# First attention of a Flamingo block: the later queries as seven half-size products instead of eight, with streamed weight sums

## Chip, cores and metric

The kernel runs on one core of one Trainium2 chip. TensorE multiplies matrices into PSUM; VectorE, ScalarE and GpSimd do the elementwise work; SP issues most DMAs. The metric is the device time of one execution in microseconds, as the median of several.

## What is computed

The reference is a two-layer gated block on x, 16 batches of 128 tokens by 512 features, all fp32. Only its first attention matters here:

```python
x = x + jnp.tanh(g_xattn[0]) * _L0_xattn_ref(_layernorm(x), ctx_512, ...)
...
q_hk = (hidden_q @ Wq.T).reshape(b, s, H, K)           # H = 16 heads
q_big = jnp.einsum('bshk,hkq->bshq', q_hk, w_kc_q)
kv_rope = kv_c * cos[None] + _rotate_half(kv_c) * sin[None]
q_r = jnp.einsum('bshq,hqr->bhsr', q_big, W_qr)        # R = 64
k_r = jnp.einsum('bld,hdr->bhlr', kv_rope, W_kr)
scores = jnp.einsum('bhsr,bhlr->bhsl', q_r, k_r)
```

Then come a softmax, the weighted sum of kv_rope, the projection back to x, a mixture-of-experts feed-forward layer, a causal attention and a second feed-forward layer.

## The kernel before

**Folding.** Up to 73 us the three query weights are multiplied into one matrix `fq` in SBUF: 4 blocks of 128 input features by 1024 columns, one column for each head and rank. The 1024 columns are 8 pairs of heads of 128 columns; `fq[:, c, ts(p, P)]` is the block of feature chunk c and head pair p. In the same way the outward weights are folded later (`fold_next`, 78 to 97 us) into `fo_raw` and `fo_sums`.

**Pairs of batches.** The 16 batches are taken as 8 pairs v = 0 to 7. The queries of pairs 0 and 1 are made during the folding with 512 tokens at a time. Those of pairs 2 to 7 come from `keys_and_queries(v)` with 256 tokens, the two batches of the pair side by side: for each of four j, two head pairs of queries (`query`, 4 matmuls of 256 columns each), the copy out of PSUM, two head pairs of keys (`key`), and their copy. `normalise` makes the normalised x, `turn` transposes it by TensorE into `turned[g]`, which two pairs share.

**Order.** Pair 2 is made in the prelude, in pieces between softmax steps. Then the loop over units u = 1 to 8 does for pair v = u-1: `gather` (weighted sums), `project` (seven products, already in the seven-product form with its sums `pair_sums`, `fo_sums`), and for pair u: `score`, `soften` (exponentials on ScalarE, scaling on GpSimd at L703), `block` (VectorE's block transposes) and `carry` (16 DMAs on SP that finish the transposition). In units 2 to 6 `keys_and_queries(u + 1)` comes last, and the next unit's `gather` and `score` follow it on TensorE. `combine_next` prepares feed-forward weights in every unit: loads and stores on SP, four sums on GpSimd (L826).

**What sets the order.** From `ordered[0] = pinned[0] = True` on, every matmul, every `send` and every VectorE instruction inside `pin` stays in program order on its engine. ScalarE's, GpSimd's and unpinned instructions, and DMAs that those engines issue, are placed by the compiler's scheduler. Each engine runs its own queue in order, so an instruction that waits holds up those behind it.

**Memory.** PSUM tiles have 512 fp32 columns; `mm_tile` has 4 buffers, `tr_tile` 2, `acc_tile` 2. Before, queries use `tr_tile`, keys `acc_tile`, scores `mm_tile`. `evacuate` alternates between VectorE (L85) and ScalarE (L87).

Of the kernel before, what the change touches and what calls it, by code (L numbers as in the profile page):

```python
# [9 lines left out]
F32 = mybir.dt.float32  # L10
AF = mybir.ActivationFunctionType
ALU = mybir.AluOpType
# [3 lines left out]
P = 128  # L16
NB = 16
D = 512
ND = D // P
GB = 4  # L20
NG = NB // GB
GT = GB * P
H = 16
NPAIR = H // 2
R = 64
# [17 lines left out]
def kernel(  # L43
# [9 lines left out]
    nc = tc.nc  # L53
# [4 lines left out]
    lnp = ctx.enter_context(tc.tile_pool(name="lnp", bufs=2))  # L58
# [16 lines left out]
    def pin(ins):  # L75
        if pinned[0]:
            tc.keep_in_program_order(ins)
# [3 lines left out]
    def evacuate(dst, src):  # L81

        flip[0] ^= 1
        if flip[0]:
            pin(nc.vector.tensor_copy(dst, src))  # L85
        else:
            nc.scalar.copy(dst, src)  # L87
# [40 lines left out]
    fq = wp.tile([P, ND, H * R], F32, tag="w16", name="fq")  # L128
# [39 lines left out]
    def matmul(*args, **kw):  # L168
        ins = nc.tensor.matmul(*args, **kw)  # L169
        if ordered[0]:  # L170
            tc.keep_in_program_order(ins)

    def transpose(*args):
        ins = nc.tensor.transpose(*args)
        if ordered[0]:
            tc.keep_in_program_order(ins)
# [29 lines left out]
    half = GT // 2  # L206
    lo, hi = slice(0, half), slice(half, GT)
    bp = ctx.enter_context(tc.tile_pool(name="f0b", bufs=1))
    wd = ctx.enter_context(tc.tile_pool(name="wd", bufs=1, space=bass.MemoryType.DRAM))
# [168 lines left out]
    with tc.tile_pool(name="a0", bufs=2) as ap, tc.tile_pool(name="a0s", bufs=3) as sp:  # L378
# [31 lines left out]
        def key(dst, p, kvT):  # L410
            matmul(dst, wkr_sb[:, ts(p, P)], kvT, start=True, stop=True)

        def query(dst, p, xnT):
            for c in range(ND):
                matmul(
                    dst, fq[:, c, ts(p, P)], xnT[:, c, :],
                    start=(c == 0), stop=(c == ND - 1),
                )

        def homes(what, v):  # L420
            twos = [
                ap.tile([P, 2, 2 * P], F32, tag=f"{what}{j}", name=f"{what}_{v}_{j}", bufs=1)
                for j in range(NPAIR // 2)
            ]
            return [t[:, i, :] for t in twos for i in range(2)], twos

        normal, xns, turned = {}, {}, {}
# [21 lines left out]
                xns[v].append(xn)  # L449

        def turn(v, which=(0, 1)):
            g, h = divmod(v, 2)
            if h == 0 and which[0] == 0:
                turned[g] = lnp.tile([P, ND, GT], F32, tag="xnT", name=f"xnT_a0_{g}", bufs=1)
            for i in which:
                xn = xns[v][i]
                tr = (acc_tile if v == 2 else tr_tile)(f"xtr_a0_{v}_{i}")
                for c in range(ND):
                    transpose(tr[:, ts(c, P)], xn[:, ts(c, P)], ident)
                dst = turned[g][:, :, ts(2 * h + i, P)]  # L460
                if v == 2:
                    pin(nc.vector.tensor_copy(dst, tr.rearrange("p (c t) -> p c t", t=P)))
                else:
                    evacuate(dst, tr.rearrange("p (c t) -> p c t", t=P))

        kvr_0 = kvT_0 = xnT_0 = None
        k_r, q_r = {0: homes("k", 0)[0]}, {0: homes("q", 0)[0]}
        for kept, tag in ((k_r, "ca"), (q_r, "cb")):  # L470
            t = ap.tile([P, NPAIR, 2 * P], F32, tag=tag, name=f"{tag}_kq", bufs=1)
# [3 lines left out]
        with tc.tile_pool(name="fold", bufs=3, side="right") as fp:  # L475
# [85 lines left out]
            for p in range(NPAIR):  # L561
# [27 lines left out]
                q_ps = tr_tile(f"q_ps0_{p}")  # L589
# [19 lines left out]
        rp = right_pools.enter_context(tc.tile_pool(name="a0r", bufs=2, side="right"))  # L609
# [57 lines left out]
        def score(b):  # L667


            v, i = divmod(b, 2)  # L670
            tiles = [mm_tile(f"s_ps{b}_{t}") for t in range(4)]
            for p in range(NPAIR):
                for j in range(2):
                    rows = slice(j * R, (j + 1) * R)
                    matmul(
                        tiles[p // 4 * 2 + j][:, ts(p % 4, P)],
                        q_r[v][p][rows, ts(i, P)], k_r[v][p][rows, ts(i, P)],
                        start=True, stop=True,
                    )
            ebs[b] = rp.tile([P, NK, H, BK], F32, tag="eb", name=f"eb_{b}")  # L680
            eTs[b] = rp.tile([P, NK, H, BK], F32, tag="eT", name=f"eT_{b}")
            soft[b] = []
            for t in range(4):
                nmx = sp.tile([P, 4], F32, tag="nmx", name=f"nmx_a0_{b}_{t}", bufs=4)
                pin(nc.vector.tensor_reduce(  # L685
                    nmx, tiles[t].rearrange("p (i l) -> p i l", l=P), AX.X, ALU.max,
                    negate=True,
                ))
                soft[b].append((tiles[t], nmx))

        def soften(b, t):
# [14 lines left out]
            soft[b][t] = e3  # L706

        def block(b, t):
            pin(nc.vector.transpose(
                ebs[b][:, :, 4 * t : 4 * t + 4, :].rearrange("p k n i -> p n k i"),  # L710
                soft[b][t].rearrange("p n (k i) -> p n k i", k=NK),
            ))
# [43 lines left out]
        def project(v, n):  # L756
# [17 lines left out]
            for i, cols in targets:  # L774
# [2 lines left out]
                    dst, y_ps, gate_x[0], dst, ALU.mult, ALU.add  # L777
                ))

        def keys_and_queries(v):  # L780
            g, h = divmod(v, 2)
            half = slice(2 * h * P, (2 * h + 2) * P)
            (k_r[v], k_two), (q_r[v], q_two) = homes("k", v), homes("q", v)
            for j in range(NPAIR // 2):
                q_ps = tr_tile(f"q_ps{v}_{j}")
                for i in range(2):
                    query(q_ps[:, ts(i, 2 * P)], 2 * j + i, turned[g][:, :, half])
                evacuate(q_two[j], q_ps.rearrange("p (i t) -> p i t", i=2))
                k_ps = acc_tile(f"k_ps{v}_{j}")
                for i in range(2):  # L790
                    key(k_ps[:, ts(i, 2 * P)], 2 * j + i, roped[g][1][:, half])
                evacuate(k_two[j], k_ps.rearrange("p (i t) -> p i t", i=2))
                yield j


# [61 lines left out]
        ups = {}  # L857

        xk = [wd.tile([P, D], F32, name=f"xk_{n}") for n in range(KEPT)]
        ordered[0] = pinned[0] = True  # L860


        def fold_next(p):
            fold_outward(p, outward[p])
            if p + 5 < NPAIR:
                outward.append(load_outward(p + 5))

        score(0)
        for p in range(7):
            fold_next(p)  # L870

            if p in (3, 5):
                turn(2, (p // 2 - 1,))
            if p % 2 == 0:
                soften(0, p // 2)
                if p:
                    block(0, p // 2 - 1)
        score(1)
        fold_next(7)
        block(0, 3)  # L880
# [3 lines left out]
        soften(1, 1)  # L884
        block(1, 0)
        pairs_2 = keys_and_queries(2)
        for t in (2, 3):
            next(pairs_2)
# [18 lines left out]
        for u in range(1, last + 1):  # L907
# [3 lines left out]
            v = u - 1  # L911
# [16 lines left out]
            if u == 1:  # L928
                now = odd
            else:  # L930
                gather(2 * v)
                if u < last:
                    score(even)
                if u + 1 < last:
                    if u % 2:
                        latents((u + 1) // 2)
                    turn(u + 1)
                if u < last - 1:
                    combine_next()
                elif u == last - 1:  # L940
                    turn_blocks(first)
# [609 lines left out]
    q = first  # L1551
    for g in range(NG):
# [40 lines left out]
        q = nxt  # L1593
# [34 lines left out]
    ap = ctx.enter_context(tc.tile_pool(name="l1", bufs=2))  # L1628
# [6 lines left out]
    for s in range(AHEAD, NB + AHEAD):  # L1635
# [38 lines left out]
        if s in (3, 5, 7):  # L1674
            n = s // 2 - 1
# [6 lines left out]
    g = NG - 1  # L1682
# [87 lines left out]
```

## Time and profile before

| what | us |
|---|---|
| median of 3 runs | 1499.63 (1497.9 to 1499.63) |
| the profiled execution | 1500.14 |
| its span, first to last instruction | 1498.3 |
| TensorE busy (granted clock 0.998) | 1477.4 |
| q_ps matmuls of 256 columns, 384 instructions, mean 379 ns, busy time | 86.9 |
| k_ps matmuls of 256 columns, 96 instructions, busy time | 24.6 |
| TensorE idle between 90 and 130 | 0.89 |
| TensorE idle between 230 and 260 | 0.00 |
| moved by DMA: SP's queue 157.13 MB, ScalarE's 0.99 MB, GpSimd's 4.13 MB | |

PE is TensorE's matmuls, PEld its weight loads, DVE VectorE, ACT ScalarE, POOL GpSimd, SPq SP's issues. L169 is the helper through which nearly all matmuls go, so groups are told apart by their tiles: `q_ps<-xnT_a,fq` are the queries. Matmul durations overlap; the time that one costs is the distance between starts. An idle time and what ended it stand in brackets. In a row of the DMA list the last number is the time from issue to landing.

### The profile page before, as it was taken

The page shows a single profiled execution, that of the slowest core. Times are in us where ns is not written, and L with a number is a line of the kernel's source. Part 1 is how long each engine was busy: PE and PEld are TensorE (multiplying, and loading weights), DVE is VectorE, ACT ScalarE, POOL GpSimd, SP SyncE. Part 2 cuts the span into 40 slices and gives each one's busy share as a digit, 9 for nine tenths or more (in the row PEclk, how much of TensorE's full clock was granted, in tenths as well). Part 3 has the DMA queues.
Part 4 walks back from the last instruction along what each step waited for, and adds up shares of the span by engine and source line. Part 5 has one row for each costly group of instructions (what it writes and reads, how often), then busy time and mean ns, then how long its engine had stood idle before and what let it go on. Part 6 is the DMA issues. An engine that isn't in the chain of part 4 may idle for free. (4 is left out here: it accounts for less than half of the span.)

```text
span 1498.3 us, 19508 instructions
## 1 busy us (share of the span) xinstructions
PE 1477.4 (99%) x6752; PEld 997.9 (67%) x6752; DVE 832.9 (56%) x1722; ACT 436.9 (29%) x1432; POOL 466.5 (31%) x500
## 2 busy tenths in 40 slices
PE   7999999999999999999999999999999999999999
PEld 5567778778877666876678666876668444444444
DVE  2274644654656555655564656455556776757422
ACT  1262432432441122012210321022203565545310
POOL 1153533623422233204320442124414333324200
PEclk9999999999999999999999999999999999999999
DMA  7533645344244822452246222721242342323212
GB/s 265 144 94 94 188 140 153 111 119 125 64 81 139 249 74 74 122 151 74 74 113 159 74 74 72 197 90 63 80 136 71 76 127 71 84 61 90 64 29 99
DMA packets 142274, 163.50 MB, mean 109 GB/s; under 512 B 54096, under 2 KB 102224, under 8 KB 140000
## 3 DMA queue, kind: packets, MB, share of 16 engines
q1 hardware_dynamic: 139024, 157.13, 36.5%
q0 software_dynamic: 2016, 4.13, 1.1%
q8 instruction: 54, 0.88, 0.3%
q10 hardware_dynamic: 1136, 0.99, 0.2%
q14 instruction: 44, 0.36, 0.1%
HBM read 106.35 MB, written 18.09 MB: 83 GB/s over the span
## 5 line engine op out<-in xcount | busy, mean ns | idle before, releaser
L1130 POOL TENSOR_TENSOR near<-base,a 128x512 f32<-128x512 f32 x32 | 42.6, 1332 | 345.0 <-ACT base L1127 233.5
L201 POOL TENSOR_TENSOR e<-e,rden_a 128x512 f32<-128x512 f32 x64 | 66.6, 1040 | 164.5 <-DVE rden_a L199 141.8
L169 PE MATMUL q_ps<-xnT_a,fq 128*128 128x256 f32 (+1 forms) x448 | 115.8, 410 | 0.0
L1127 ACT ACTIVATE a<-a 128x512 f32<-128x512 f32 x64 | 40.3, 630 | 256.8 <-DVE a L1126 256.8
L169 PE MATMUL l_ps<-t,b_sb 128*128 128x512 f32 x256 | 115.1, 592 | 0.0
L696 ACT ACTIVATE e<-s_ps,nmx_a 128x128 f32<-128x128 f32 x256 | 90.2, 386 | 78.0 <-DVE nmx_a L685 40.4
L194 ACT ACTIVATE e<-e,nmx_a 128x128 f32<-128x128 f32 x256 | 98.8, 387 | 34.7 <-DVE nmx_a L189 34.7
L1126 DVE TENSOR_TENSOR a<-l_ps,base 128x512 f32<-128x512 f32 x64 | 44.0, 688 | 108.0 <-PE l_ps L169 107.9
L169 PEld LDWEIGHTS q_ps<-xnT_a,fq 128*128 128x128 f32 x448 | 84.8, 190 | 24.5 <-issue 12.5
L703 POOL TENSOR_TENSOR e<-e,rden_a 128x512 f32<-128x512 f32 x64 | 66.0, 1039 | 100.7 <-DVE rden_a L701 100.7
L169 PEld LDWEIGHTS l_ps<-t,b_sb 128*128 128x128 f32 x256 | 48.6, 190 | 59.5 <-issue 57.6
L169 PE MATMUL fy_ps<-ring,far 128*128 128x256 f32 x384 | 87.2, 380 | 0.0
L169 PE MATMUL y_ps<-fo_raw,c 128*128 128x256 f32 x384 | 85.8, 380 | 0.9 <-DVE c L85 0.9
L776 DVE SCALAR_TENSOR_TENSOR x<-y_ps,gates,x 128x256 f32<-128x256 f32 x112 | 48.7, 477 | 67.0 <-PE y_ps L169 66.9
L1192 DVE SCALAR_TENSOR_TENSOR x<-fy_ps,gw,x 128x256 f32<-128x256 f32 x112 | 46.5, 475 | 69.3 <-PE fy_ps L169 69.3
L169 PEld LDWEIGHTS fy_ps<-ring,far 128*128 128x128 f32 x384 | 72.6, 190 | 13.6 <-issue 4.0
L169 PEld LDWEIGHTS y_ps<-fo_raw,c 128*128 128x128 f32 x384 | 72.3, 190 | 10.7 <-ACT c L87 1.0
L1344 DVE STREAM_TRANSPOSE eb<-e 128x512 f32<-128x512 f32 x64 | 45.5, 712 | 42.0 <-POOL e L201 37.4
L169 PE MATMUL ht_ps<-T,ring 128*128 128x256 f32 x256 | 65.7, 379 | 0.0
L169 PE MATMUL t_ps<-a,a_sb 128*128 128x512 f32 x128 | 65.4, 592 | 0.0
L169 PE MATMUL t_ps<-base,a_sb 128*128 128x512 f32 x128 | 65.4, 592 | 0.0
L169 PE MATMUL y_ps<-fo_sums,c 128*128 128x256 f32 x256 | 60.4, 385 | 2.1 <-ACT c L87 0.8
(257 smaller groups left out, 2956.3 us busy)
## 6 DMA issues: line engine op xcount, KB each, us to landing
ring<-w SPq DMA_DIRECT2D x32, 896.0 KB, 4.5
eT<-eb SPq DMA_DIRECT2D x312, 64.0 KB, 2.0
ring<-w SPq DMA_DIRECT2D x16, 1024.0 KB, 5.3
ring<-in_f_w SPq DMA_DIRECT2D x12, 1024.0 KB, 6.1
wq<-in_wq SPq DMA_DIRECT2D x8, 512.0 KB, 6.1
x<-in_x SPq DMA_DIRECT2D x16, 256.0 KB, 4.6
quarters<-in_f_w SPq DMA_DIRECT2D x32, 128.0 KB, 2.5
w<-sums SPq DMA_DIRECT2D x8, 512.0 KB, 3.6
```

Of the source, the lines that this page charges most:

```text
L169: ins = nc.tensor.matmul(*args, **kw)
L194: nc.scalar.activation(dst[:, ts(i, P)], src[:, ts(i, P)], AF.Exp, bias=nmx[:, i : i + 1], accum_out=den[:, i : i + 1],)
L201: nc.gpsimd.tensor_tensor(d3, d3, rden.unsqueeze(2).to_broadcast([P, 4, P]), ALU.mult)
L696: nc.scalar.activation(e[:, ts(i, P)], s_ps[:, ts(i, P)], AF.Exp, bias=nmx[:, i : i + 1], accum_out=den[:, i : i + 1],)
L703: nc.gpsimd.tensor_tensor(e3, e3, rden.unsqueeze(2).to_broadcast([P, 4, P]), ALU.mult)
L776: pin(nc.vector.scalar_tensor_tensor(dst, y_ps, gate_x[0], dst, ALU.mult, ALU.add))
L1126: nc.vector.tensor_tensor(a, l_ps, base, ALU.add)
L1127: nc.scalar.activation(a, a, AF.Gelu_apprx_tanh)
L1130: nc.gpsimd.tensor_tensor(mix, base, second, ALU.add)
L1192: nc.vector.scalar_tensor_tensor(dst, y_ps[:, ts(i, half)], q.first[:, t : t + 1], dst, ALU.mult, ALU.add,)
L1344: nc.vector.transpose(by_blocks(ebs[b])[:, :, 4 * j : 4 * j + 4, :].rearrange("p k n i -> p n k i"), e.rearrange("p (n k i) -> p n k i", n ...
```

## The change

The product of the 512 input features by 1024 query columns over the two batches of a pair is split into halves on each side: two halves of the features, two of the columns (`near_q`, `far_q`), and the two batches. The eight block products become seven, with sums of blocks on both sides: four sums of the transposed x (in `turn`), four sums of blocks of `fq` (`query_sums`, once), and sums of the results on the way out of PSUM (`query_product`). Each product has 4 x 2 written matmuls with 128 columns streamed, where before a pair had 32 with 256.

Two of the seven weight blocks stay in `fq` (its near half). The other five are stored in DRAM once (`fq_kept`) and read back for each pair, in the order 4, 5, 3, 2, 6, into the far half of `fq`, which makes two slots (feature rows 0-1 and 2-3). Each read is two DMAs of 256 KB on ScalarE's queue, issued after the product that used the slot. The q of a pair becomes one tile, the transposed x one tile for each pair. Pair 2 uses `tr_tile`, later pairs `mm_tile`. The order of products and key steps is 4, 0, key, 5, 1, key, 3, key, 2, key, 6 for pairs 3 to 7 and key, 4, 0, key, 5, 1, key, 3, key, 2, 6 for pair 2.

```diff
 def turn(v, which=(0, 1)):
-    g, h = divmod(v, 2)
-    if h == 0 and which[0] == 0:
-        turned[g] = lnp.tile([P, ND, GT], F32, tag="xnT", name=f"xnT_a0_{g}", bufs=1)
+    if which[0] == 0:
+        turned[v] = lnp.tile([P, 2, ND, 2 * P], F32, tag="xnT", name=f"xnT_a0_{v}", bufs=1)
...
+    if which[-1] == 1:
...
+        pin(nc.vector.tensor_tensor(t_1, b12, b11, ALU.subtract))
+        pin(nc.vector.tensor_tensor(t_2, b22, t_1, ALU.subtract))
+        nc.gpsimd.tensor_tensor(t_3, b22, b12, ALU.subtract)
+        nc.gpsimd.tensor_tensor(t_4, b21, t_2, ALU.subtract)
+        turned[v] = [b11, b21, t_4, t_1, t_2, t_3, b22]
...
+streamed = (4, 5, 3, 2, 6)
...
+def query_sums():
+    a11, a12 = fq[:, :2, near_q], fq[:, 2:, near_q]
+    a21, a22 = fq[:, :2, far_q], fq[:, 2:, far_q]
+    two = rp.tile([P, 2, 2, H * R // 2], F32, tag="eT", name="fq_sums")
+    s_1, s_2 = two[:, 0], two[:, 1]
+
+    def keep(n, src):
+        for h in range(2):
+            begin = nc.sync if n in (2, 5) else nc.gpsimd
+            begin.dma_start(out=fq_kept[n, h], in_=src[:, :, ts(h, 2 * P)])
+
+    keep(2, a22)
+    nc.gpsimd.tensor_tensor(s_1, a21, a22, ALU.add)
+    nc.vector.tensor_tensor(a21, a11, a21, ALU.subtract)
+    keep(5, a21)
+    nc.gpsimd.tensor_tensor(s_2, s_1, a11, ALU.subtract)
+    keep(3, s_1)
+    keep(4, s_2)
+    nc.gpsimd.tensor_tensor(a22, a12, s_2, ALU.subtract)
+    keep(6, a22)
...
+def fetch():
+    n = len(fetched)
+    if n == 5 * (NB // 2 - 2):
+        return
+    rows = slice(n % 2 * 2, n % 2 * 2 + 2)
+    for h in range(2):
+        near_end = H * R // 2 + h * 2 * P
+        nc.scalar.dma_start(
+            out=fq[:, rows, near_end : near_end + 2 * P],
+            in_=fq_kept[streamed[n % 5], h],
+        )
+    fetched.append(fq[:, rows, far_q])
...
+def query_product(v, n, q, u_2):
+    if n < 2:
+        w = fq[:, 2 * n : 2 * n + 2, near_q]
+    else:
+        w = fetched[used[0]]
+        used[0] += 1
+    ps = (tr_tile if v == 2 else mm_tile)(f"q_ps{v}_{n}")
+    for m in range(NPAIR // 2):
+        for c in range(2):
+            matmul(
+                ps[:, ts(m, P)], w[:, c, ts(m, P)], turned[v][n][:, c],
+                start=c == 0, stop=c == 1,
+            )
+    src = ps.rearrange("p (m t) -> p m t", t=P)
+    c11, c12, c21, c22 = [q[:, 4 * m : 4 * m + 4, i] for m in range(2) for i in range(2)]
+    if n == 4:
+        nc.scalar.copy(u_2, src)
+    elif n == 0:
+        pin(nc.vector.tensor_tensor(u_2, src, u_2, ALU.add))
+        nc.scalar.copy(c11, src)
+    elif n == 5:
+        pin(nc.vector.tensor_tensor(c21, src, u_2, ALU.add))
+    elif n == 1:
+        pin(nc.vector.tensor_tensor(c11, src, c11, ALU.add))
+    elif n == 3:
+        nc.scalar.copy(c22, src)
+        nc.gpsimd.tensor_tensor(c12, c22, u_2, ALU.add)
+        nc.gpsimd.tensor_tensor(c22, c22, c21, ALU.add)
+    else:
+        dst = c21 if n == 2 else c12
+        pin(nc.vector.tensor_tensor(dst, src, dst, ALU.add))
+    if n > 1:
+        fetch()
...
 def keys_and_queries(v):
...
-    for j in range(NPAIR // 2):
-        q_ps = tr_tile(f"q_ps{v}_{j}")
-        for i in range(2):
-            query(q_ps[:, ts(i, 2 * P)], 2 * j + i, turned[g][:, :, half])
-        evacuate(q_two[j], q_ps.rearrange("p (i t) -> p i t", i=2))
+    u_2 = lnp.tile([P, NPAIR // 2, P], F32, tag="xn", name=f"u2_{v}")
+    for j, ns in enumerate(((4, 0), (5, 1), (3,), (2, 6))):
+        if v > 2:
+            query_product(v, ns[0], q, u_2)
+            if j < 2:
+                query_product(v, ns[1], q, u_2)
         k_ps = acc_tile(f"k_ps{v}_{j}")
...
+        if v == 2:
+            query_product(v, ns[0], q, u_2)
+        if j == 3 or v == 2 and j < 2:
+            query_product(v, ns[1], q, u_2)
         yield j
...
+query_sums()
 ordered[0] = pinned[0] = True
...
 score(0)
 for p in range(7):
     fold_next(p)
...
+for _ in range(2):
+    fetch()
 score(1)
```

More of the change, by code (lines that the diff above doesn't have):

```diff
@@ L420, in homes @@
         def homes(what, v):
+            if what == "q":
+                whole = ap.tile([P, NPAIR, 2, P], F32, tag="q", name=f"q_{v}", bufs=1)
+                return [whole[:, p].rearrange("p i t -> p (i t)") for p in range(NPAIR)], whole
             twos = [
@@ L459, in turn @@
                     transpose(tr[:, ts(c, P)], xn[:, ts(c, P)], ident)
-                dst = turned[g][:, :, ts(2 * h + i, P)]
+                dst = turned[v][:, 0, :, ts(i, P)]
                 if v == 2:
@@ L464, in turn @@
                     evacuate(dst, tr.rearrange("p (c t) -> p c t", t=P))
+            if which[-1] == 1:
+                b11, b12, b21, b22 = [
+                    turned[v][:, 0, 2 * k : 2 * k + 2, ts(i, P)]
+                    for k in range(2) for i in range(2)
+                ]
+                t_1, t_2, t_3, t_4 = [
+                    turned[v][:, 1, n].rearrange("p (c t) -> p c t", t=P) for n in range(4)
+                ]
+                pin(nc.vector.tensor_tensor(t_1, b12, b11, ALU.subtract))
[3 more added lines that the diff above has]
+                turned[v] = [b11, b21, t_4, t_1, t_2, t_3, b22]
         kvr_0 = kvT_0 = xnT_0 = None
@@ L778, in project @@
                 ))
+        streamed = (4, 5, 3, 2, 6)
+        fq_kept = {
+            (n, h): wd.tile([P, 2, 2 * P], F32, name=f"fq_{n}_{h}")
+            for n in streamed for h in range(2)
+        }
+        near_q, far_q = slice(0, H * R // 2), slice(H * R // 2, H * R)
+        def query_sums():
[16 more added lines that the diff above has]
+            keep(6, a22)
@@ new lines @@
+        fetched = []
+        def fetch():
[10 more added lines that the diff above has]
+            fetched.append(fq[:, rows, far_q])
+        used = [0]
@@ L782, in keys_and_queries @@
             half = slice(2 * h * P, (2 * h + 2) * P)
-            (k_r[v], k_two), (q_r[v], q_two) = homes("k", v), homes("q", v)
-            for j in range(NPAIR // 2):
-                q_ps = tr_tile(f"q_ps{v}_{j}")
-                for i in range(2):
-                    query(q_ps[:, ts(i, 2 * P)], 2 * j + i, turned[g][:, :, half])
-                evacuate(q_two[j], q_ps.rearrange("p (i t) -> p i t", i=2))
+            (k_r[v], k_two), (q_r[v], q) = homes("k", v), homes("q", v)
+            u_2 = lnp.tile([P, NPAIR // 2, P], F32, tag="xn", name=f"u2_{v}")
[4 more added lines that the diff above has]
+                        query_product(v, ns[1], q, u_2)
                 k_ps = acc_tile(f"k_ps{v}_{j}")
```

## The prediction

> **What bounds the kernel now.** I read the page's busy shares first, then its chain, then the stretches around the change, then the order of events in one of them, and last the rows that price what is new.
>
> ```profile
> span 1498.3 us, 19508 instructions
> PE 1477.4 (99%) x6752; PEld 997.9 (67%) x6752; DVE 832.9 (56%) x1722; ACT 436.9 (29%) x1432; POOL 466.5 (31%) x500
> ...
> PE 12%; DVE 1%; POOL 0%; ACT 0%; DMA 0%; issue 0%; SPq 0%; POOLq 0%; ACTq 0%
> ```
>
> TensorE is busy 99% of the span; the chain breaks off after 13% of it, but what it follows is TensorE. So a microsecond off TensorE counts, unless a wait takes its place. The next view gives busy time per stretch: 78 to 97 us is the folding of the outward weights, 243 to 260.4 us the keys and queries of pair 4 (units u=2 to 6 make pairs 3 to 7).
>
> ```profile
> core 0: us, PE busy (x) PEld busy (x) DVE busy (x) ACT busy (x) POOL busy (x), PEclk, DMA share, GB/s
> 78.00:97.00 19.00, 19.00 (x95) 10.57 (x94) 16.84 (x40) 12.80 (x56) 13.92 (x18) 1.00 0.29 84
> ...
> 243.00:260.40 17.40, 17.40 (x82) 15.33 (x81) 4.69 (x9) 2.64 (x5) 0.91 (x2) 1.00 0.52 148
> ```
>
> In the second, VectorE, ScalarE and GpSimd are mostly idle: a good place for extra sums. In the first, VectorE has 2.2 us free of 19.
>
> The same 17.4 us in order of time (start, length, engine):
>
> ```profile
> 243.19 3.62 PE L169 MATMUL q_ps<-xnT_a,fq 128*128 128x256 f32 x16
> ...
> 246.64 1.03 PE L169 MATMUL k_ps<-kvT,wkr_sb 128*128 128x256 f32 x4
> 246.84 0.59 ACT L87 COPY q<-q_ps 128x512 f32<-128x512 f32 x1 [0.43 <-PE q_ps L169]
> 247.51 3.62 PE L169 MATMUL q_ps<-xnT_a,fq 128*128 128x256 f32 x16
> ...
> 254.61 1.08 SPq L179 DMA_DIRECT2D xk<-x  x2
> ...
> 260.05 1.41 POOL L826 TENSOR_TENSOR sums<-quarters 128x256 f32<-128x256 f32 x2 [16.49 <-DMA w<-sums]
> ```
>
> A written matmul is two instructions here: 8 written ones make the x16. From start to next start 16 take 246.64-243.19 = 3.45 us, 216 ns each, though one lasts 379 (pipelined). A key step takes 247.51-246.64 = 0.87. A pair is 4 x (3.45+0.87) = 17.3 us, 13.8 of it queries.
>
> **What comes off TensorE.** The new scheme has per pair 7 products x 4 x 2 written matmuls with 128 columns streamed, so 16 instructions a product. The nearest row is the fold's f_ps, also fp32, 128 columns, a weight load for each:
>
> ```profile
> 70.53 1.95 PE L546 MATMUL f_ps<-m,wq 128*128 128x128 f32 x16
> 72.32 1.02 PE L169 MATMUL k_ps<-kvT,wkr_sb 128*128 128x512 f32 x2
> ```
>
> 16 in 72.32-70.53 = 1.79 us (112 ns each). Seven products take 12.53, so 13.80-12.53 = 1.27 us per pair and **7.6 us over six pairs** (2 to 7). Bounds: the three groups before it took 1.89 (57.05 to 58.94), which leaves 0.57 per pair, 3.4 in all; exactly half of 3.45 would give 1.72 per pair, 10.4. I take 7.6, from the only one of these groups with no other shape's weights switched in ahead.
>
> The Trainium skill's page "TensorE: Matmul & The Clock Gate", section "Back-to-back issue gap", gives about 81 ns for each load-and-multiply pair at 128 columns. With it a product would take 1.30 us, a pair 9.1, and the six would save 28 us. The f_ps row has 112 ns in this kernel, and the row decides.
>
> **What is added beside it.** Per pair VectorE gets 5 sums at 0.69 (the base sum of a 128x512 accumulator, 688 ns) and 2 sums of 128x256 at about 0.42 (the fo_sums row), 4.3 us, and gives up some q copies; ScalarE 3 copies of 0.59 for up to 4, and 10 DMA issues of 0.45 (wkr_sb on its queue), 4.5; GpSimd 2 sums at 1.33 and 2 at 0.73, 4.1. In the 17 us stretch these have 12 us or more free each: nothing, while that cover holds. Without it the part of 4.3 us that VectorE is late would hold up the next unit's gather copies and the score behind them. The single home for q is no new wait: the scores that read the last one end before the stretch.
>
> **The fetch for the sixth sum.** Streamed weights use two slots in turn. Order on TensorE: 4, 0, key, 5, 1, key, 3, key, 2, key, 6. The weights of 3 and 2 go out behind 4 and 5 and have 7 and 5.3 us. Those of 6 take the slot of 3, so they can go only when 3 is done, behind ScalarE's copy of it: 0.20 to the copy (246.64 to 246.84), 0.59 copy, then the landing time L of the first half (256 KB); the second is 0.45 later and needed 0.9 later. TensorE covers key + product 2 + key = 0.87+1.79+0.87 = 3.53. Wait per pair: 0.79+L-3.53 = **L-2.74**. For pair 2 the order ends 3, key, 2, 6: cover 2.66, wait L-1.87. Behind the waiting TensorE stand gather and score of the next unit; its sequence is fixed, so nothing fills the hole. Rows for L (KB each, us to landing):
>
> ```profile
> x<-in_x SPq DMA_DIRECT2D x16, 256.0 KB, 4.6
> ...
> quarters<-in_f_w SPq DMA_DIRECT2D x16, 256.0 KB, 3.3
> ...
> xk<-x SPq DMA_DIRECT2D x8, 256.0 KB, 2.3
> ```
>
> The ends are 2.3 and 4.6. I take 3.3: loads of that size, issued two together, in this very part of the kernel. Waits: 5 x 0.56 + 1.43 = **4.2 us** (0.4 at 2.3; 12.0 at 4.6).
>
> The Trainium skill's page "DMA: Bandwidth & Descriptors", section "Anatomy of one DMA — SWDGE (gpsimd) path", fits 2.0 us plus bytes over 436 KB/us, 2.6 us for 256 KB; its section "Issuing engines are not separate DMA queues" says that ScalarE's queue shares the 16 engines with SP's. By the first the waits would sum to 0.7 us; the second speaks for more, since SP's xk, quarters and sums (1.4 MB) leave from 254.61 on, within 0.2 us of the fetch. The quarters row, taken amid SP's own traffic, stands between.
>
> **The start.** The query weights are complete at 72.52+0.37 = 72.9 us. GpSimd then makes three sums of 128x1024 (2.35 each at L746) and issues six DMAs; its own issues cost 1.64/3 = 0.55 (three of eT at 1138.15): 72.9+7.05+3.3 = 83.2 us. Its first instruction today is at 81.37, with none idle until 95.84:
>
> ```profile
> 81.37 0.73 POOL L639 TENSOR_TENSOR fo_sums<-fo_raw,fo_sums 128x256 f32<-128x256 f32 x1 [38.32 <-ACT fo_raw L633]
> ...
> 97.76 0.73 POOL L639 TENSOR_TENSOR fo_sums<-fo_raw,fo_sums 128x256 f32<-128x256 f32 x1 [1.92 <-ACT fo_raw L633]
> ```
>
> So its queue is 1.9 us late; the softmax scalings in it release VectorE's block transposes, which stand in a fixed order with the copies that free the fold's accumulators, and for those TensorE waits next. VectorE also gets one 128x1024 difference, 1.2 us (L745). Bounds: 0 (GpSimd's 1.92 us hole at 97.76 takes it up) to 13 (issue growing with bytes, 2.2 each, plus VectorE). SP's and ScalarE's issues do not grow so, hence the low price: 1.9+1.2 = **3.1 us**. SP's four stores wait only for the weights and the difference, ahead of the wo loads at 80.71. SP's carries get ScalarE's loads beside them: the first gather has some 2.5 us over them (last issue about 111, landing 113, gather 115.48), the later ones 10 or more: nothing.
>
> **Sum.** -7.6 + 4.2 + 3.1 = -0.3 us. The profiled execution took 1500.14 (span 1498.3 and 1.84 around it), so 1499.8 there; it lies 0.5 above the median 1499.63, so 1499.3 for a median. A measurement here tells about 0.2% (3 us) from no change.
>
> **Rivals.**
> *A, my sum: the gain is given back*, 1499.3, its own range 1496 to 1503; 0.37.
> *B, the covers hold.* L about 2.5 and GpSimd's hole takes the start: 0+0.6+1: -7.6+1.6 = -6.0, 1493.6. For: the 128 KB quarters land in 2.5, ScalarE's queue is otherwise empty in these stretches. Against: 512 KB go in one burst. 0.25.
> *C, slower: the sixth fetch is late.* At L = 4.6 the waits are 12.0, and with the start 3.1 the sum is +7.5: 1507.1. Place: before product 6 of each pair. The sum is 6L-20.1 (six waits -15.6, -7.6, +3.1): no change at L = 3.35, 3 us slower at 3.85. For: x and kv of 256 KB took 4.6 and 3.8, beside SP's quarters and sums. Against: quarters at 3.3. 0.28.
> *D, slower: GpSimd's order.* Product 3's two sums stand behind the L826 sums, which today wait 16.49 us for a DMA until 260.05, 16.9 into the stretch. Then 16.9+2.9+2.7+1.4 = 23.9 until q is ready, while the score wants it at 16.0+3.5 = 19.5: 4.4 x 5 pairs on top, about 1521. Against: the sums' operands are ready 5 us ahead of L826's. 0.05.
> *E, shorter streams gain less than they say*: 1.89 a product, 3.4 saved in place of 7.6: 1503.5. 0.05.
>
> **Numbers.** Faster by over 0.2%: 0.05 of A and 0.24 of B, 0.29. Within: 0.28 of A, 0.01 each of B, C, 0.02 of E: 0.32. Slower: 0.04 of A, 0.27 of C, 0.05 of D, 0.03 of E: 0.39. The range 1492.5 to 1511 takes in B, A, E and most of C.
>
> **What would show it.** The q_ps groups x16 at 1.79 start to start; an idle gap of TensorE ended by a DMA into fq ahead of the last query product, 0.6 us in pairs 3 to 7, 1.4 in pair 2; GpSimd's L639 beginning near 83 and o_ps waiting for VectorE before 97 us. Gaps above 1.5 us speak for C, none for B, score waiting for q for D. I am wrong if the two slots do not make the sixth fetch wait, or if the start costs over 6 us.

## The result and the profile after

The changed kernel takes 1519.38 us (median of 4 runs, 1518.8 to 1521.48) where the kernel before, run beside it, takes 1499.41 (1497.9 to 1499.63). The ratio is 1.0138, 95% interval 1.012 to 1.0155: slower by 1.4%.

Line numbers moved with the change: the softmax scaling L703 is now L718, the block transpose L709 is L724, the feed-forward sums L826 are L925, the sums in `project` L776 are L791, and the start's L639 is L654.

The head of the page of the changed kernel, and two rows of its DMA list (the last number is the median from issue to landing):

```profile
span 1517.7 us, 20328 instructions
PE 1477.5 (97%) x7040; PEld 1004.5 (66%) x7040; DVE 856.0 (56%) x1753; ACT 440.3 (29%) x1438; POOL 500.8 (33%) x533
...
fq<-fq ACTq DMA_DIRECT2D x60, 256.0 KB, 4.1
...
w<-sums SPq DMA_DIRECT2D x8, 512.0 KB, 4.3
```

TensorE's busy time is the same to 0.1 us, and the span is 19.4 longer. (A busy time that doesn't shrink is no proof that nothing was saved: here the products do take less, and matmuls at a lower clock, shown below, take it back.) The stores `w<-sums` landed in 3.6 us before, in 4.3 now.

Where the 19.4 went is read from the distance between the first query matmuls of successive pairs, in one profiled execution of each kernel. These are worked out from the timelines; "start" is from the first score to the first query of the loop, "four" the sum of the next four units, "last" from the last queries to the attention's end.

| kernel | start | the four units | four | last |
|---|---|---|---|---|
| before | 111.49 | 54.99, 54.12, 54.45, 54.01 | 217.57 | 91.59 |
| after | 117.19 | 61.68, 55.44, 58.27, 58.40 | 233.79 | 90.16 |

So +5.7 in the start, +16.2 in the four units, -1.4 in the last; the rest before and behind these stretches is 1.1 shorter, and 5.7+16.2-1.4-1.1 = 19.4. The last unit has the new products too, but no feed-forward sums behind them, and it is the one that gains what a pair was to gain.

What TensorE waited for in the changed kernel (total, times, longest):

```profile
PE c_ps L169 <- DVE x L791: 9.6, 3, 3.6
...
PE k_ps L169 <- ACT kvT L87: 3.1, 1, 3.1
...
PE q_ps L169 <- DMA fq<-fq: 2.1, 3, 0.8
```

None of the three is among the rows of the kernel before. The last is the wait that the forecast was about; it is a tenth of the loss. The first is in the middle of the units, 20 us behind the changed stretch. This is how one looks in order of time, GpSimd, then VectorE, then TensorE, in the first of the four units (queries from 193.31):

```profile
205.18 1.27 POOL L866 TENSOR_TENSOR q<-q,u 128x512 f32<-128x512 f32 x1 [8.20 <-ACT q L865]
...
218.16 1.41 POOL L925 TENSOR_TENSOR sums<-quarters 128x256 f32<-128x256 f32 x2 [10.36 <-DMA w<-sums]
...
224.86 0.72 POOL L925 TENSOR_TENSOR sums<-quarters 128x256 f32<-128x256 f32 x1 [2.87 <-DMA w<-sums]
...
228.27 2.04 POOL L718 TENSOR_TENSOR e<-e,rden_a 128x512 f32<-128x512 f32 x2
```
```profile
229.35 0.71 DVE L724 STREAM_TRANSPOSE eb<-e 128x512 f32<-128x512 f32 x1 [6.69 <-POOL e L718]
229.98 0.44 DVE L791 SCALAR_TENSOR_TENSOR x<-y_ps,gates,x 128x256 f32<-128x256 f32 x1
```
```profile
230.48 1.12 PE L169 MATMUL c_ps<-eT,kvr 128*128 128x512 f32 x2 [3.58 <-DVE x L791]
232.62 6.54 PE L169 MATMUL y_ps<-fo_sums,c 128*128 128x256 f32 x16 [1.01 <-ACT c L87]
```

GpSimd does two groups of feed-forward sums, and the even batch's softmax scalings stand behind both. The second group waits for a store of earlier sums to land. VectorE stands idle 6.69 us for the scaling, and behind its transpose, in fixed order, stands the sum L791 that frees the accumulator TensorE needs. TensorE stands 3.58 us for that. Its next 16 matmuls take 6.54 us where 3.72 is usual (the same product at 241.07). From 231.53 to 238.36 us the clock granted to TensorE was 0.50, and two more such stretches follow in the four units, each behind one of the three waits for L791 (of the last three numbers the first is the granted clock):

```profile
core 0: us, PE busy (x) PEld busy (x) DVE busy (x) ACT busy (x) POOL busy (x), PEclk, DMA share, GB/s
231.53:238.36 6.83, 5.82 (x15) 4.58 (x15) 4.53 (x7) 1.03 (x3) 2.29 (x3) 0.50 0.18 42
347.59:351.00 3.41, 3.41 (x9) 2.70 (x10) 2.69 (x4) 0.04 (x1) 1.02 (x1) 0.50 0.10 24
405.61:409.02 3.41, 2.85 (x7) 2.35 (x8) 2.79 (x5) 0.70 (x2) 1.04 (x1) 0.50 0.00 0
```

Of the 6.54 us, 5.74 lie in the first stretch and count half, 2.87, and with the other 0.80 that is 3.67. So this wait cost more than its own length. TensorE was busy for 12.1 us of the three stretches, which is some 6.0 us lost to the clock (an estimate), beside 15.7 us of idle time in the four units. The kernel before has 1.1 us of idle time there and a granted clock of 1.00. How the loss divides between waits and clock can differ from run to run: the mean clock was 0.993 in two of the four runs and 0.996 in the others, at about the same time.

The same place in the kernel before (queries from 188.20):

```profile
208.63 1.42 POOL L826 TENSOR_TENSOR sums<-quarters 128x256 f32<-128x256 f32 x2 [17.48 <-issue]
...
216.44 1.41 POOL L826 TENSOR_TENSOR sums<-quarters 128x256 f32<-128x256 f32 x2 [4.91 <-DMA w<-sums]
...
219.30 2.04 POOL L703 TENSOR_TENSOR e<-e,rden_a 128x512 f32<-128x512 f32 x2
```

The order is the same. Counted from the queries, the first group came at 20.4 and comes at 24.9 now, and the scaling at 31.1 and 35.0. The store that the first group waits for was issued on SP at +16.7 and landed in 3.6 (at 208.51, just ahead of the group, though the row names no releaser); now it is issued at +18.1 and takes 6.7. SP's queue shows why it is later (waits of SP from 185 or 190 to 450 us, first the kernel before, then after):

```profile
SPq L179 <- DMA w<-quarters: 12.7, 6, 3.1
```
```profile
SPq L179 <- DMA w<-quarters: 17.2, 6, 4.3
SPq L179 <- DMA fq<-fq: 10.4, 11, 2.2
...
SPq L179 <- DMA eT<-eb: 2.9, 5, 1.0
```

SP, which issues no fetch in the loop and uses none of its data, waits 10.4 us for fetches to complete.

### The profile page after: what moved, and what is told of

It is laid out like the page before. It is cut to its first block, busy times and chain, and to the rows that moved or that the text cites. A ratio compares the mean times of both kernels' runs of the same rounds, so it can differ in the third digit from the quotient of the medians.

```text
span 1517.7 us, 20328 instructions
## 1 busy us (share of the span) xinstructions
PE 1477.5 (97%) x7040; PEld 1004.5 (66%) x7040; DVE 856.0 (56%) x1753; ACT 440.3 (29%) x1438; POOL 500.8 (33%) x533
## 3 DMA queue, kind: packets, MB, share of 16 engines
q1 hardware_dynamic: 140112, 158.18, 35.5%
## 5 line engine op out<-in xcount | busy, mean ns | idle before, releaser
L169 PE MATMUL q_ps<-xnT_a,fq 128*128 128x128 f32 (+1 forms) x736 | 109.8, 303 | 2.2 <-DMA fq<-fq 2.1
L169 PEld LDWEIGHTS q_ps<-xnT_a,fq 128*128 128x128 f32 x736 | 91.9, 192 | 19.1 <-issue 12.6
L718 POOL TENSOR_TENSOR e<-e,rden_a 128x512 f32<-128x512 f32 x64 | 66.3, 1045 | 68.1 <-DVE rden_a L716 68.1
L791 DVE SCALAR_TENSOR_TENSOR x<-y_ps,gates,x 128x256 f32<-128x256 f32 x112 | 48.7, 476 | 66.2 <-PE y_ps L169 66.0
L169 PE MATMUL y_ps<-fo_sums,c 128*128 128x256 f32 x256 | 65.5, 412 | 6.6 <-DVE rden_a L716 2.8
L1446 DVE STREAM_TRANSPOSE eb<-e 128x512 f32<-128x512 f32 x64 | 45.5, 712 | 40.8 <-POOL e L201 37.7
L724 DVE STREAM_TRANSPOSE eb<-e 128x512 f32<-128x512 f32 x64 | 44.4, 694 | 42.2 <-POOL e L718 42.0
L169 PE MATMUL c_ps<-eT,kvr 128*128 128x512 f32 x128 | 58.5, 595 | 9.6 <-DVE x L791 9.6
L169 PEld LDWEIGHTS y_ps<-fo_sums,c 128*128 128x128 f32 x256 | 51.7, 207 | 23.1 <-ACT c L87 8.4
```

The lines of the kernel that those rows point to most:

```text
L718: nc.gpsimd.tensor_tensor(e3, e3, rden.unsqueeze(2).to_broadcast([P, 4, P]), ALU.mult)
L724: pin(nc.vector.transpose(ebs[b][:, :, 4 * t : 4 * t + 4, :].rearrange("p k n i -> p n k i"), soft[b][t].rearrange("p n (k i) -> p n k i", ...
L791: pin(nc.vector.scalar_tensor_tensor(dst, y_ps, gate_x[0], dst, ALU.mult, ALU.add))
L1446: nc.vector.transpose(by_blocks(ebs[b])[:, :, 4 * j : 4 * j + 4, :].rearrange("p k n i -> p n k i"), e.rearrange("p (n k i) -> p n k i", n ...
```

## The experiments

The theory after this reading: the fetches (and the new sums on GpSimd) make the feed-forward sums late, and that reaches TensorE because the softmax scalings stand behind them on GpSimd. The rivals: the fetches as such (bytes, number, waits in ScalarE's queue); the extra sums; the sixth fetch. All results in one table. The time is the median, the ratio is to the kernel before beside it, and columns are as above.

| run | time, us | ratio (95%) | start | four | last |
|---|---|---|---|---|---|
| e1 no fetch | 1504.18 (1 run) | | 118.63 | 217.04 | 89.80 |
| e2 small fetch | 1515.86 (1 run) | | 119.95 | 227.14 | 89.80 |
| e3 scalings first | 1500.65 | 1.0011 (1.0001 to 1.002) | 116.38 | 212.58 | 90.60 |
| e4 sums on VectorE | 1517.87 (1 run) | | 119.95 | 228.43 | 90.52 |
| e5 before, scalings first | 1497.31 | 0.9994 (0.9985 to 1.0003) | 110.94 | 217.14 | 91.11 |
| e6 = e3, kv transposes early | 1497.14 | 0.999 (0.9981 to 0.9999) | 116.10 | 213.56 | 90.32 |
| e7 = e6, half sums later | 1496.98 | 0.9993 (0.9983 to 1.0003) | 115.85 | 213.54 | 90.24 |
| e8 before, with transfers | 1510.16 | 1.0079 (1.0059 to 1.01) | 112.19 | 226.15 | 92.21 |
| e9 merged fetch | 1523.38 | 1.0163 (1.0145 to 1.0182) | 118.98 | 234.25 | 90.64 |
| e10 = e7, two more edits | 1497.88 | 0.9995 (0.9986 to 1.0004) | 115.19 | 212.87 | 90.15 |
| e11 = e10, a sum on VectorE | 1495.2 | 0.9979 (0.9969 to 0.9988) | 115.31 | 213.54 | 89.80 |
| e12 = e8, scalings first | 1505.77 | 1.0046 (1.0031 to 1.0061) | 111.50 | 222.60 | 91.49 |
| e13 = e3, no fetch | 1497.58 | 0.9992 (0.9983 to 1.0002) | 118.03 | 211.91 | 89.78 |

Five starts hold a stretch at a granted clock of 0.50: e1 3.41 us from 100.64, e2 6.83 from 99.31, e4 6.83 from 99.50, e9 3.41 from 117.08, e13 3.41 from 101.65. They account for 1.7 to 3.0 us of these starts (estimates), most of what the starts of e1, e2, e4 and e9 have over the changed kernel's 117.19 and that of e13 over e3's. It is not an effect of the edits as far as is shown: TensorE's wait for kvT near 98 us was 3.1 us in the changed kernel, e1, e2, e3 and e13 alike, and such a stretch came with it in e1, e2 and e13 alone.

**e1, no fetch.** 28 of the 30 fetches are left out; later products use what the slots hold.

```diff
-            for h in range(2):
+            for h in range(2 if n < 2 else 0):
```

> Leaves out the fetches of the streamed weight sums after the first two (28 of 30): pairs 2 to 7 multiply by whatever stands in the two slots. Everything else stays. Theory T (fetch traffic): the 14.7 MB on ScalarE's queue slow the SP transfers that land beside them, so the feed-forward sums on GpSimd (L925) get their data late and the softmax scalings (L718) behind them too; then units 3, 5 and 6 lose their 5 to 8 us each no more, and the time falls from 1519 to 1496-1503 (the start's loss of some 6 us stays, the products save 7.6). Rival L (load): the added sums on GpSimd and VectorE make the delay themselves; then the time stays at 1512 or above.

1504.18, just above the theory's range: the four units fall by 16.8 us to 217.04, the start does not shrink. The fetches cause most of the units' loss. But 217.04 is still only 0.5 below the kernel before, where four pairs' products should have saved 5: something else costs there as well.

**e2, an eighth of the bytes**, the same number of transfers and the same waits; the products use weights that are partly old.

```diff
+            few = 2 * P if n < 2 else 32
...
-                    out=fq[:, rows, near_end : near_end + 2 * P],
-                    in_=fq_kept[streamed[n % 5], h],
+                    out=fq[:, rows, near_end : near_end + few],
+                    in_=fq_kept[streamed[n % 5], h][:, :, :few],
```

> Fetches 32 of 256 columns in each DMA after the first two, an eighth of the bytes, with the same number of DMAs at the same places; the products multiply by partly old columns. Theory T by bytes: within 4 us of the kernel without fetches, 1496 to 1505. Rival W (waits): ScalarE's and SP's queues hold each other up through the completions that each DMA waits for before it is issued, whatever its size; then it stays at 1510 or above. Rival L: 1512 or above.

1515.86, as rival W had it (rival L's number too, but e1 had fallen far below that). Of the 16.8 us that the fetches cost in the four units, the bytes carry 6.7 (233.79 to 227.14); 10.1 stay.

**e9, half the number**: one transfer of 512 KB for two of 256.

```diff
-            for h in range(2):
-                near_end = H * R // 2 + h * 2 * P
-                nc.scalar.dma_start(
-                    out=fq[:, rows, near_end : near_end + 2 * P],
-                    in_=fq_kept[streamed[n % 5], h],
-                )
+            nc.scalar.dma_start(out=fq[:, rows, far_q], in_=fq_kept[streamed[n % 5]])
```

> The changed kernel with each fetch as one transfer of 512 KB in place of two of 256 KB: same bytes, half as many transfers on ScalarE's queue, product 6's first half waiting for the whole of its weights. Theory (most of the loss goes with the number of transfers and what waits for their issue and completion, as the run with an eighth of the bytes gave back only 3.5 us): units 2 us shorter on the mean, 1508 to 1514. Rival (time on the 16 engines decides): 1518 to 1521.

1523.38, the units at 234.25: no gain, and TensorE's own wait for fetches rose from 2.1 to 6.4 us. The theory that the loss goes with the number of transfers is wrong, and the time lies above the rival's range too. Neither bytes nor number sets it alone; how the delay on SP's side is shared between its waits and longer landings stays open.

**e4, the two late half sums t_3, t_4 on VectorE** instead of between GpSimd's two groups.

> The whole change, but the third and fourth sums of the transposed x (L477, L478) are made on VectorE and not on GpSimd, where they stand 1.46 us ahead of the first softmax scaling. Theory T: 4 to 6 us faster than the change (1513 to 1516), since the DMA's part of the delay stays. Rival L: 1505 or below.

1517.87, above the theory's range. The units take 5.4 us less and the start 2.8 more, some 2.1 of that by the clock stretch named above. The GpSimd work that the change adds counts, and is the lesser part.

**e3, the order alone.** The whole change, but in units 2 to 6 GpSimd does the even batch's scalings ahead of the second group of feed-forward sums.

```diff
-                if u < last - 1:
-                    combine_next()
-                elif u == last - 1:
+                if u == last - 1:
                     turn_blocks(first)
...
             soft_step(now, 4)
+            if 1 < u < last - 1:
+                behind[0] = True
+                combine_next()
+                behind[0] = False
             pair_sums(v)
```

(`behind` and a test in `soften` pin both groups of GpSimd's instructions to this order.)

> The whole change, but in units 2 to 6 GpSimd does the softmax scalings of the even batch ahead of the second group of feed-forward sums (that group is moved behind them and both are kept in program order). If the loss runs through that order on GpSimd, units 3, 5 and 6 lose 1 to 2 us in place of 5 to 8 and the time is 1502 to 1508. If VectorE waits for something else (ScalarE's copies of the transposed x, the eT carries), it stays at 1512 or above.

1500.65, below the theory's range, the units at 212.58: 21.2 us less with every fetch and every sum still there. TensorE's idle time in them falls from 15.7 to 0.9 us, and the granted clock is 1.00 throughout; these two, 14.8 and some 6.0, make up nearly all of it. GpSimd in the first of the units (queries from 192.98):

```profile
218.50 1.41 POOL L927 TENSOR_TENSOR sums<-quarters 128x256 f32<-128x256 f32 x2 [11.38 <-DMA w<-sums]
...
222.72 2.04 POOL L718 TENSOR_TENSOR e<-e,rden_a 128x512 f32<-128x512 f32 x2
...
228.47 0.73 POOL L927 TENSOR_TENSOR sums<-quarters 128x256 f32<-128x256 f32 x1
```

The first group is as late as before this edit, 25.5 after the queries. The scaling comes at 29.7 instead of 35.0, and the second group, at 35.5, holds up nobody.

**e5, the same order in the kernel before.**

> The kernel before, with only GpSimd's order changed: in units 2 to 6 the even batch's four softmax scalings stand ahead of the second group of feed-forward sums. Theory (the order costs only because the change makes the sums' data late): before, the second group's data came in time, so little is there to gain; 1496 to 1501, units of 54 to 55 us as now. Rival (the order is a loss of its own that was always there): each unit shortens by 2 us or more, 1490 or less, and the repair of the changed kernel is then a gain that has nothing to do with the change.

1497.31, interval across 1: within 0.2%. The order was no loss until the change made the data late.

**e13, e3 without the fetches.**

> The changed kernel with GpSimd's scalings first (1500.7) and 28 of the 30 fetches left out, so that later products multiply by whatever the two slots hold. Theory (with that order the fetches cost only the sixth fetch's waits, about 2 us): 1498 to 1500. Rival (fetches cost 15 us whatever the order, as the run without them in the old order gave): 1490 or less.

1497.58, just below the theory's range. The four units take 211.91, only 0.67 less than with the fetches. With the one order the fetches cost 16.8 us in these units, with the other 0.7. And 217.14 (e5) less 211.91 gives the products' worth without any fetch: 1.31 us per pair.

**e8, the transfers alone**, in the kernel before: ten stores of 256 KB per pair on ScalarE's queue, to memory that nobody reads. (The fetches are loads.)

```diff
                 evacuate(q_two[j], q_ps.rearrange("p (i t) -> p i t", i=2))
+                for h in range(4 if j == 3 else 2):
+                    nc.scalar.dma_start(out=junk[2 * j + h], in_=q_two[j])
```

> The kernel before, with ten transfers of 256 KB more per pair on ScalarE's queue (stores of the q that was just copied out, to memory that nobody reads), at the places where the change has its fetches; products, sums and order stay as before. Theory (the fetches, through the waits and landings that they share with SP's transfers, make the feed-forward sums late on GpSimd): 1508 to 1516, the units longer by 2 to 5 us, with VectorE's transposes waiting for GpSimd. Rival (the half-size products' extra work on GpSimd, VectorE and ScalarE makes them late): 1498 to 1502.

1510.16: without a new product or sum, the units grow by 8.6 us. That is the theory's time, but only in part its way: TensorE's longest waits (from 185 to 500 us) are for ScalarE's copies of k, and VectorE's L776 comes second.

```profile
PE c_ps L169 <- ACT k L87: 4.1, 2, 3.0
PE c_ps L169 <- DVE x L776: 1.4, 1, 1.4
```

**e12, e8 with the scalings first.**

> The kernel before with the ten extra transfers per pair on ScalarE's queue (1510.2 alone) and GpSimd's softmax scalings ahead of the second feed-forward sums (1497.3 alone). Theory (late transfers reach TensorE only through the order on GpSimd): most of the 12 us goes, 1497 to 1502. Rival (they reach it through ScalarE's copies of k, which stood behind waits for these transfers and held TensorE up for 4.4 us): 1504 to 1509.

1505.77, in the rival's range: 4.4 of 11.8 us come back. Two units are exactly at e5's 54.12 and 54.45, but the first stays at 58.67 and the last is 1.4 longer. There another path is at work (waits of TensorE and of ScalarE from 185 to 500 us):

```profile
PE c_ps L169 <- ACT k L87: 3.3, 2, 2.3
```
```profile
ACT k L87 <- DMA junk<-q: 24.1, 5, 6.9
```

ScalarE's copies of k stand in its queue behind its own transfers, which wait for completions of earlier ones. So the transfers have a second way to TensorE. In e3 ScalarE's k copies wait 9.3 us for fetches, but TensorE has no such row; there the second way is covered.

**e6, e7, e10, e11: the start.** In e3 the start is still 4.9 us longer than before. It showed VectorE late, then this wait (the changed kernel, VectorE, GpSimd and TensorE):

```profile
74.16 3.35 DVE L448 TENSOR_SCALAR xn_a<-x,mv_a,rstd_a 128x512 f32<-128x512 f32 x2
...
77.77 1.21 DVE L815 TENSOR_TENSOR fq<-fq 128x1024 f32<-128x1024 f32 x1
```
```profile
74.82 2.41 POOL L817 TENSOR_TENSOR fq_sums<-fq_sums,fq 128x1024 f32<-128x1024 f32 x1
...
84.02 0.98 POOL L654 TENSOR_TENSOR fo_sums<-fo_raw,fo_sums 128x256 f32<-128x256 f32 x1
```
```profile
82.92 1.96 PE L169 MATMUL o_ps<-wo,wckv_all 128*128 128x512 f32 x4 [1.11 <-issue]
...
100.26 1.13 PE L169 MATMUL k_ps<-kvT,wkr_sb 128*128 128x256 f32 x4 [3.07 <-ACT kvT L87]
```

The same two normalisations take 1.00 us in the kernel before. VectorE is then late with the maxima of the second score (behind the half sums t_1, t_2 besides, 1.9 us), ScalarE's exponentials wait for these, and its copy of kvT stands behind the exponentials. e6 issues `latents(1)` ahead of `score(1)`:

```diff
             fetch()
+        latents(1)
         score(1)
...
         soften(1, 0)
-        latents(1)
```

> The changed kernel with the scalings first (1500.7), and the transposes of kv for pairs 2 and 3 issued ahead of the second score instead of behind it, so that ScalarE's copy of kvT no longer stands behind exponentials that wait for VectorE's late maxima. Theory (the start loses mainly the 3.1 us for which TensorE waits for kvT): score to first loop query shrinks from 116.4 to 113 or 114 and the time to 1497 to 1498. Rival (VectorE is late in any case and the next wait takes its place): 1499.5 to 1501.

e7 moves the four half sums of pair 2 behind `score(1)`:

> As the run with the early kv transposes, and besides the four half sums of pair 2's transposed x go behind the second score's maxima instead of ahead of them. Theory (these sums, 1.9 us on VectorE, are the other part of its lateness): the stretch falls to about 112.5 and the time to 1495 to 1497, below the kernel before by 0.1 to 0.3%. Rival (nothing waits for the maxima any longer once kvT is early, or the product that needs the sums now waits for them): as that run or up to 1 us longer.

e10 makes pair 2's two copies of the transposed x on ScalarE and ends that pair with product 2, key, product 6:

> As e7_start_mended, and pair 2's two copies of the transposed x go to ScalarE (1.4 us off VectorE), and pair 2's last steps become product 2, key, product 6 as in later pairs, so that the key covers part of the sixth fetch. Theory (VectorE's lateness and the sixth fetch's 1.2 us are what is left of the start's loss): score to first loop query 113.5 to 114.5, 1494.5 to 1496. Rival (another wait takes their place): 1496.5 to 1497.5.

e11 makes the first query sum with `nc.vector.tensor_tensor` instead of GpSimd's:

> As e10_start_mended2, and the first query sum runs on VectorE, which waits 1.4 us for ScalarE there, instead of on GpSimd (2.4 us). Theory (in the kernel after, VectorE's two normalisations took 3.35 us instead of 1.00 while GpSimd made its sums; less of GpSimd's sums beside them, less of that): they take under 2.5 us, GpSimd's fold sums begin 1 to 2 us earlier, the time is 0.5 to 1.5 us below e10. Rival (the slowdown follows whatever sum of GpSimd runs then, and VectorE's 1.2 us come on top): as e10 or up to 1 us above.

Each shrank a wait that it aimed at, and together they shortened the start by no more than 1.2 us: 116.10, 115.85, 115.19, 115.31. After e6 TensorE waits 1.1 us for VectorE's fold sums (L653) and 1.4 us for the sixth fetch in place of the 3.1 for kvT; after e7, 1.2 for a half sum; after e10 the sixth fetch costs 0.6 and the half sum 1.8. So the rivals were right about the stretch: another wait takes over each time. The times of e6 and e7 came out where the theory had them, some 3.5 us below e3, but their profiles show only 1.3 and 3.2 us less, part of it outside the start (ahead of the first score the granted clock was 0.50 for 10.2 us in e3's profile, 6.8 in e6's and not at all in e7's); a share of that is the scatter between kernels, and it is not claimed for the edits. e10's own time lies above both its ranges. e11 is 0.9979 of the kernel before: faster by 0.2%, the best version here. Its normalisations are undisturbed again, and another instruction of VectorE is slow instead (GpSimd's L822 ran from 73.43 to 75.79):

```profile
74.29 2.57 DVE L820 TENSOR_TENSOR fq<-fq 128x1024 f32<-128x1024 f32 x1 [0.55 <-PE q_ps L169]
...
76.98 1.00 DVE L448 TENSOR_SCALAR xn_a<-x,mv_a,rstd_a 128x512 f32<-128x512 f32 x2
```

That is the rival's condition (the slowdown follows whatever sum of GpSimd runs then), though not its time. Why e11 is 2.7 us below e10 with the same start stays open; e10's profiled execution was 3.9 us longer behind the first attention, where no edit is, some 1.7 of it by 3.41 us at a granted clock of 0.50 from 1224.63.

## Why the prediction was wrong

**The products: right.** Two products are 32 instructions, from their start to that of the key behind them:

```profile
193.31 3.73 PE L169 MATMUL q_ps<-xnT_a,fq 128*128 128x128 f32 x32
196.88 1.03 PE L169 MATMUL k_ps<-kvT,wkr_sb 128*128 128x256 f32 x4
```

3.57 us, 1.79 each, as the f_ps row gave. The saving per pair was put at 1.27; e13 against e5 shows 1.31. Rival E (1.89 a product) falls.

**"What is added beside it … nothing, while that cover holds": this step failed**, and with it the look at SP's queue, which stopped at "SP's carries … nothing". The carries did land in time (no gather waited for one); the stores of feed-forward sums behind them on that queue did not. The cover was judged in the 17 us in which the work is added, where the engines are idle, and not where the queues go next. The row quoted for rival D, GpSimd's L826 waiting 16.49 us for a DMA, was the warning: an engine that waits on a DMA has no free time to give, it has a due time. SP's stores of earlier sums are what it waits for, and SP now waits for fetches. The scalings, block transposes, L791 and TensorE hang on that in fixed order. In place of 0 the four units lost 21.2 us (e3 against the changed kernel; 14.8 idle, some 6.0 by the clock), 5.1 of it without the fetches (217.04 in e1 against 211.91 in e13). The text says what late work on VectorE would hold up ("the next unit's gather copies"), but did not ask what stands behind late sums on GpSimd.

**Rival D had the queue and not the victim.** It gave 1521, close to the 1519.38 measured, for another reason: product 3's two sums were to stand behind the feed-forward sums. They run 13 us ahead of them (205.18 against 218.16), for the reason the text gave against D. What stands behind is the softmax scaling. The number is a coincidence.

**The sixth fetch: 4.2 predicted, 2.1 measured**, by two errors against each other. The changed kernel, the pair of the table's first unit:

```profile
207.49 1.09 PE L169 MATMUL q_ps<-xnT_a,fq 128*128 128x128 f32 x8
209.38 1.16 PE L169 MATMUL q_ps<-xnT_a,fq 128*128 128x128 f32 x8 [0.80 <-DMA fq<-fq]
```

The first half of the weights was issued at 203.95, as product 3 ended, not behind ScalarE's copy (0.79 earlier), and landed in 3.4, near the 3.3 taken. The second half was issued 1.41 later, not 0.45, behind a completion that its issue waited for, and that half is the one that was late. Only pairs 2 to 4 waited. Rival C (long landings, 4.6) falls: the median over all fetches was 4.1, but the first halves for product 6 landed in 3.1 to 3.8. B falls too: the covers did not hold.

**The start: 3.1 predicted, 6.3 measured** (117.19-111.49, plus the 1.27 that pair 2 was to save, less its sixth fetch of 0.69), over the 6 that the forecast named as a sign of being wrong. TensorE's idle time there rose from 2.1 to 8.1 us. GpSimd's queue late was right: "L639 beginning near 83", measured 84.02; and VectorE's 1.2 us difference took 1.21. Missing were 2.35 us on the normalisations beside GpSimd's sum, and the half sums of pair 2, 1.9 us on VectorE (0.79 and 1.14, priced at 0.42 each), counted where VectorE is idle and not here, where the text itself says that it has 2.2 us free of 19.

**The sum by the measured terms**: products -7.9 (six pairs at 1.31, as four showed it), sixth fetch +2.1, start +6.3, and the late chain of the four units 20.0 (their 16.2, plus 5.2 that the products save there, less 1.4 of fetch waits): 20.5, less the 1.1 of the stretches before and behind: 19.4.

## What to carry to other kernels

An engine whose idle time ends with a DMA is not free: look up which store or load releases it, on which queue that is issued, what is put into that queue or beside it, and what stands behind the waiting instruction on its engine and the next. Before adding transfers or sums to such a queue, move urgent work ahead of the instruction that waits; here that order alone was worth nothing before the change and 19 us after it. When a stretch is late, removing the wait that shows may only uncover the next one, as e6, e7 and e10 did in the start. And look at the granted clock behind a wait of TensorE: here it added some 6 us to 15.7 us of idle time.

## What the runs showed of the hardware

SP's queue waited for transfers of ScalarE's queue and the other way round, with no data between them: 10.4 us for fetches on SP from 190 to 450 us, and on ScalarE a copy of k that stood behind fetches waiting for SP:

```profile
205.36 4.36 ACTq L832 DMA_DIRECT2D fq<-fq  x3
209.76 0.59 ACT L87 COPY k<-k_ps 128x512 f32<-128x512 f32 x1 [4.65 <-DMA eT<-eb]
```

ScalarE was idle for 4.65 us there; the product to be copied was done some 2 us before the copy (it began at 206.62 and took 1.03). A completion semaphore is the counter by which a transfer tells that it has landed. In the trace the transfers of both queues share eight of them from 190 to 450 us, and in these rows an issue that gets one waits until its last user has landed: an eT of SP was issued at 205.56 and landed at 209.11, the fetch that takes over its semaphore left at 209.19, and the copy of k came at 209.76. Long landings on one queue are so passed to the other.

Two groups of VectorE's instructions with SBUF operands ended only after a 128x1024 sum of GpSimd that ran beside them: 3.35 in place of 1.00 us (to 77.51, the sum to 77.23), and 2.57 in place of 1.21 in e11 (to 76.86, the sum to 75.79). The Trainium skill's page "GPSIMD Engine Reference", section "1. Specifications", has GpSimd's SBUF interface shared with VectorE for instructions in a two-port mode or with two SBUF inputs; the row of e11, a sum with two SBUF inputs, agrees with it. Whether the normalisations ran in a two-port mode no run here shows. The forecast had not drawn on it.

GpSimd's queue took 2.98 us to issue four transfers of 256 KB, 0.75 each, and 1.40 for two, where three of 64 KB had cost 0.55 each.
